# Layer 0 of a four-layer graph network: copies of nodes on ScalarE, later weights and transposes at other gates, another order of norms

## The chip, the cores and the metric

The kernel runs on one core of a Trainium2 chip. A core has a matrix engine (TensorE, in the profile PE, with its weight loads PEld), VectorE (DVE), ScalarE (ACT), GpSimd (POOL) and SyncE (SP), which here only issues DMAs. Each engine works through its own queue in order. They meet through semaphores. The metric is device microseconds of one execution, from the launch's start to its end.

## The reference, cut to what matters

The input `x` is 128 samples of 64 nodes with 256 features. Four layers follow each other, each as `x = x + layer(relu(layernorm(x)))`. The change lies in layer 0, which is two graph convolutions and then four LSTMs over windows of nodes:

```python
h = relu(einsum('ts,bsh->bth', adj, x @ Wg0 + bg0))
h = relu(einsum('ts,bsh->bth', adj, h @ Wg1 + bg1))
for p in range(1, 5):
    nw = 64 // p
    wins = h[:, :nw * p, :].reshape(B * nw, p, 256)
    last = lstm_last(Wih[p-1], Whh[p-1], bih[p-1], bhh[p-1], wins)   # gates i, f, g, o
    h = h.at[:, arange(nw) * p + (p - 1), :].set(last.reshape(B, nw, 256))
```

So a window of `p` nodes is read by `p` LSTM steps, and the last hidden state is written back in the place of the window's last node. The next `p` reads what the one before it wrote. Layers 1 to 3 (attention over edges, a graph convolution with batch norms, dense attention) are not touched.

## The kernel before

The 8192 rows (128 samples by 64 nodes) are cut into 16 chunks of 512 and 4 groups of 2048. All is 32-bit float. Layer 0 has two stages.

The first stage is `graph_convolutions(n)`, a generator for each chunk with five steps: the norm of the chunk (`Norm(...).all()`), the aggregation with the adjacency matrix, the two products with weights, and the second aggregation. A loop starts one generator in each round and takes every generator under way one step on, the oldest first, and from the fourth round on also one step of the generators that make tables for the later layers (`edge_tables`, `late_tables`). `Norm` takes statistics on DVE (L87, L88), then the root and the shift: for chunk 0 with a square root on ScalarE and two small instructions on DVE (L95 to L97), for the others with four small instructions on POOL (L99 to L102). Then four activations on ScalarE write the normed rows (L109). The results of the first half of the chunks stay in SBUF (`hTs0`, shown as `hT`), those of the second half go to DRAM (`hmem`).

The second stage runs the LSTMs. It has two halves of two groups each, `ga` and `gb`, and in each half four phases, one for each window length 1 to 4. A phase is a list of `Step`s: one time step `t` of one part of the nodes. Two parts alternate, so that one step's hidden state can be made while the other one multiplies. A step has three gates at `t` = 0 (nothing is fed back yet) and four after. The product of 256 by 256 features is done in 2x2 blocks by seven products instead of eight (a scheme of Strassen and Winograd): for this, weights and operands have to be summed and subtracted ahead. `Weights` loads 1 MB of weights on SP and makes four sums on POOL (L417): `wih` and `sih` for the input, in two buffers, `whh` and `shh` for the fed-back state, in one. `Step.prepare` makes the operands of a step (`xop`, two buffers): two copies of nodes on POOL (L606 and L607, for window length 1 not needed) and three subtractions on DVE (L608, L614, L615).

A gate's seven products go into three banks of PSUM: `pa` (three buffers), `pb` (two, shared with `bank`) and `pc` (three). Products 1, 6, 5 and 3 run into `pa` one after the other. Between them ScalarE reads `pa` (L668 after 1, L673 after 6) and DVE (L678 after 5), so the next product waits for that reader. The activations are L653, the tanh of the cell is L705. `gate` is a generator in four parts, and a loop over slots interleaves three gates: in a slot the newest gate runs products 1 and 2, the one before it product 5, the oldest 3 and 4, and the newest 6 and 7. So a gate is done two slots after it began. The last multiplication of a window's last step (L718) writes the nodes back.

In the same loop `prepare` of the next step is called in a step's next to last gate, `phase_over` loads later weights once a phase's last gate is done, and `group_out` is called for both chunk pairs of a group when its last step of window length 4 is done: it transposes the group back on TensorE (L152, 16 transposes for each chunk pair, which here is `c` = 0 or 1), adds it to the residual `x` (L155, loaded to `xres` by `fetch_x`), stores it to `xa` from POOL's queue, and loads the second half's `hT` over it from `hmem` on SP.

The order in each queue is not simply that of the text: a scheduler places instructions when it expects their operands and buffers to be ready, and takes the earlier one of the text where several are ready. `late(ins)` pins an instruction to its place in the order of the text.

Of the kernel before, what the change touches and what calls it, by code (L numbers as in the profile page):

```python
# [13 lines left out]
ALU = mybir.AluOpType  # L14
# [9 lines left out]
NEG = -1.0e30  # L24
# [6 lines left out]
def gnn_stack_kernel(ctx: ExitStack, tc: tile.TileContext, a: dict, out: bass.AP):  # L31
    nc = tc.nc
    NTOK = out.shape[0]
    NCH = NTOK // CHUNK
# [36 lines left out]
    def late(ins):  # L71

        tc.keep_in_program_order(ins)
# [72 lines left out]
    def add_transposed(xt, i0, src, col):  # L146

        p = bank()
        for i2 in range(2):
            for c in range(2):  # L150
                k = (i2 * 2 + c) * P
                nc.tensor.transpose(  # L152
                    p[:, k : k + P], src[:, c, col + i2 * P : col + (i2 + 1) * P], ident
                )
        nc.vector.tensor_tensor(  # L155
            xt[:, i0 : i0 + 2, :],
            p.rearrange("p (i d) -> p i d", i=2),
            xt[:, i0 : i0 + 2, :],
            ALU.add,
        )  # L160
# [9 lines left out]
    def late_tables():  # L170
        with ExitStack() as setup:
            s2 = setup.enter_context(tc.tile_pool(name="s2", bufs=1, side="right"))
            nc.sync.dma_start(out=wext[:, :, :D], in_=a["W3"])
            w3T = s2.tile([P, 2, D], F32, tag="w3T", name="w3T")
            nc.sync.dma_start(out=w3T, in_=a["W3T"])
            a3 = s2.tile([P, 2, 2], F32, tag="a3", name="a3")
            nc.sync.dma_start(out=a3, in_=a["a3"])

            nc.vector.tensor_scalar(mask3, adj2, 0.0, NEG, ALU.is_equal, ALU.mult)
            yield  # L180

            eye = s2.tile([P, T], F32, tag="eye", name="eye")
            for h in range(2):
                r = slice(h * T, (h + 1) * T)
                nc.vector.tensor_copy(eye[r, :], ident[r, r])
            an = s2.tile([P, T], F32, tag="an", name="an")
            anT = s2.tile([P, T], F32, tag="anT", name="anT")
            nc.vector.tensor_tensor(an, adj2, eye, ALU.add)
            nc.vector.tensor_tensor(anT, adjT2, eye, ALU.add)
            yield  # L190
            deg = s2.tile([P, 3], F32, tag="deg", name="deg")
            diag = s2.tile([P, T], F32, tag="diag", name="diag")
            nc.vector.tensor_tensor(diag, an, eye, ALU.mult)
            nc.vector.tensor_reduce(deg[:, 0:1], anT, AX.X, ALU.add)
            nc.vector.tensor_reduce(deg[:, 1:2], an, AX.X, ALU.add)
            nc.vector.tensor_reduce(deg[:, 2:3], diag, AX.X, ALU.add)
            yield
            dinv = s2.tile([P, 1], F32, tag="dinv", name="dinv")
            nc.vector.tensor_tensor(dinv, deg[:, 0:1], deg[:, 1:2], ALU.add)
            nc.vector.tensor_tensor(dinv, dinv, deg[:, 2:3], ALU.subtract)  # L200
            nc.gpsimd.tensor_tensor(dinv, dinv, half_power[:, 0:1], ALU.pow)
            yield
            dinv_b = s2.tile([P, P], F32, tag="dinv_b", name="dinv_b")
            nc.vector.tensor_copy(dinv_b, dinv.to_broadcast([P, P]))
            nc.vector.memset(bdH, 0.0)
            nc.vector.tensor_scalar(anT, anT, dinv, None, ALU.mult)
            yield
            p = bank()
            mm(p[:, :T], dinv_b[:T, :], ident[:T, :T])
            yield  # L210
            for h in range(2):
                r = slice(h * T, (h + 1) * T)
                nc.vector.tensor_tensor(bdH[r, r], p[r, :T], anT[r, :], ALU.mult)
            yield

            p = bank()
            for c in range(2):
                for k in range(2):
                    mm(
                        p[:, 2 * c : 2 * c + 2],  # L220
                        w3T[:, k, c * P : (c + 1) * P],
                        a3[:, k, :],
                        k == 0,
                        k == 1,
                    )
            yield
            for c in range(2):
                nc.vector.tensor_copy(wext[:, c, D:], p[:, 2 * c : 2 * c + 1])
                nc.vector.tensor_copy(wa2[:, c, :], p[:, 2 * c + 1 : 2 * c + 2].to_broadcast([P, T]))
            yield  # L230
# [160 lines left out]
    with ExitStack() as l0:  # L391
# [35 lines left out]
        weights = {}  # L427


        with ExitStack() as conv:  # L430
# [37 lines left out]
            nc.sync.dma_start(out=bias2, in_=a["bhh"])  # L468
            for h in range(2):
                r = slice(h * T, (h + 1) * T)  # L470
                nc.vector.tensor_copy(bdA[r, r], adjT2[r, :])

            rsum = wc.tile([P, T], F32, tag="rsum", name="rsum")
            p = bank()
# [3 lines left out]

            def graph_convolutions(n):

                h = Norm(coming.pop(n), n == 0).all()
                if 4 <= n + 3 < NCH:
                    coming[n + 3] = load_x(n + 3)
                yield
# [53 lines left out]
            for n in range(NCH + 4):  # L538
                if n < NCH:
                    under_way.append(graph_convolutions(n))  # L540
                for one in list(under_way):
                    if next(one, 0) == 0:
                        under_way.remove(one)
                    if n >= 3:
                        next(tables, None)
                if n == 2:
                    weights["ih", 0], weights["ih", 1] = Weights("ih", 1), Weights("ih", 2)
                    weights["hh", 1] = Weights("hh", 2)
                    nc.vector.tensor_tensor(bias, bias, bias2, ALU.add)
# [19 lines left out]
        class Step:  # L569
# [21 lines left out]
            def prepare(self):  # L591

                N, t = self.N, self.t
                x = xop.tile([P, 7 * NMAX], F32, tag="x", name="xop")
                if self.w == 1:
                    v = x[:, : 4 * N].rearrange("p (q n) -> p q n", n=N)
                    nc.vector.tensor_tensor(
                        v[:, 0:2], self.nodes(slice(2, 4), 0), self.nodes(slice(0, 3, 2), 0), ALU.subtract
                    )
                    b11, b21, b22 = (self.nodes(slice(k, k + 1), 0)[:, 0] for k in (0, 1, 3))  # L600
                    nc.vector.tensor_tensor(v[:, 2], b22, v[:, 0], ALU.subtract)
                    nc.vector.tensor_tensor(v[:, 3], b21, v[:, 2], ALU.subtract)
                    self.x = {1: b11, 2: b21, 3: b22, 4: v[:, 3], 5: v[:, 0], 6: v[:, 2], 7: v[:, 1]}
                    return
                v = x[:, : 7 * N].rearrange("p (q n) -> p q n", n=N)
                nc.gpsimd.tensor_copy(self.as_nodes(v[:, 0:2]), self.nodes(slice(0, 2), t))  # L606
                nc.gpsimd.tensor_copy(self.as_nodes(v[:, 2:3]), self.nodes(slice(3, 4), t))  # L607
                nc.vector.tensor_tensor(  # L608
                    self.as_nodes(v[:, 3:5]),
                    self.nodes(slice(2, 4), t),  # L610
                    self.nodes(slice(0, 3, 2), t),
                    ALU.subtract,
                )
                nc.vector.tensor_tensor(v[:, 5], v[:, 2], v[:, 3], ALU.subtract)  # L614
                nc.vector.tensor_tensor(v[:, 6], v[:, 1], v[:, 5], ALU.subtract)  # L615
                self.x = {1: v[:, 0], 2: v[:, 1], 3: v[:, 2], 4: v[:, 6], 5: v[:, 3], 6: v[:, 5], 7: v[:, 4]}
# [160 lines left out]
        def phase_over(ph):  # L777

            if ph + 2 < len(phases):
                weights["ih", ph + 2] = Weights("ih", phases[ph + 2])  # L780
            nxt = ph + 1 if ph + 1 < len(phases) and phases[ph + 1] > 1 else ph + 2
            if phases[ph] > 1 and nxt < len(phases):
                weights["hh", nxt] = Weights("hh", phases[nxt])

        tasks = [(s, q, k) for s in range(len(steps)) for k, q in enumerate(steps[s].gates)]
        flight = []
        later = []
        norm_steps = iter(())
        steps[0].prepare()
        for slot in range(len(tasks) + 2):  # L790
# [16 lines left out]
            if new:  # L807
                next(one)
                flight.append((new, one))
                at, k = new[0], new[2]  # L810
                if k == len(step.gates) - 2 and at + 1 < len(steps):
                    steps[at + 1].prepare()
                if step.w == MAX_SKIP and step.t == 2 and k < 2:
                    for u in range(2):
# [2 lines left out]
            while later and later[0][0] <= slot:  # L817
                _, kind, n = later.pop(0)
                residual[n] = fetch_x(n)
            next(norm_steps, None)  # L820
            if old:
                (at, q, k), step = old[0], steps[old[0][0]]
                if k == len(step.gates) - 1:
# [10 lines left out]
                            norms1[n] = Norm(xt)  # L834
                        norm_steps = first_norms1(norms1)
                    if step.w == MAX_SKIP and step.t == MAX_SKIP - 1:
                        for c in range(2):
                            group_out(step.g, c)
        for _ in norm_steps:
            pass  # L840
    psums["banks"] = None
    w12 = ctx.enter_context(tc.tile_pool(name="w12", bufs=1, side="right"))
    xin1 = l01.enter_context(tc.tile_pool(name="xin1", bufs=2, side="right"))
# [667 lines left out]
```

## Time and profile before

| | us |
|---|---|
| median of three runs (lowest to highest) | 2181.02 (2179.18 to 2182.44) |
| the profiled execution | 2181.59 |
| its span, first to last instruction | 2179.8 |

The stages by time, with the busy time of each engine in them (us, from the same execution):

| from to | what | PE | DVE | ACT | POOL | granted PE clock |
|---|---|---|---|---|---|---|
| 0 to 34 | start of the convolutions | 21.36 | 17.35 | 9.46 | 17.49 | 0.95 |
| 34 to 206 | convolutions | 172.00 | 113.48 | 68.31 | 26.64 | 1.00 |
| 206 to 763 | LSTMs, first half | 538.91 | 324.95 | 296.27 | 84.88 | 0.98 |
| 763 to 1311 | LSTMs, second half | 531.00 | 321.31 | 293.83 | 85.21 | 0.98 |
| 1311 to 2180 | layers 1 to 3 | 811.90 | 493.32 | 426.17 | 200.32 | 0.94 to 0.98 |

How to read it: PE is busy nearly all the time, so what a change can win on the other engines counts only where PE stands still for it, or where the granted clock falls below 1 because PE stood still. A matmul on 256 columns is recorded as two instructions of 0.216 us each at full clock.

### The profile page before, as it was taken

How to read it: one execution, taken by the hardware profiler on the slowest of the kernel's cores; microseconds unless marked ns; L12 is line 12 of the kernel's file. 1: busy time of each engine (PE TensorE's matmuls, PEld its weight loads, DVE VectorE, ACT ScalarE, POOL GpSimd, SP SyncE). 2: the span in 40 equal slices, each digit the busy share in tenths (PEclk: the TensorE clock that was granted, in tenths of full speed). 3: DMA queues.
4: the chain of work that ended last, by engine and by line, in shares of the span. 5: the costliest groups of instructions: out<-in, count | busy, mean ns of one | idle time of the engine just before them, and what ended most of it. 6: DMA issues, size and time to landing. Idle time of an engine off the chain costs nothing.

```text
span 2179.8 us, 25495 instructions
## 1 busy us (share of the span) xinstructions
PE 2075.2 (95%) x9508; PEld 1373.7 (63%) x9508; DVE 1270.4 (58%) x2281; ACT 1094.0 (50%) x2079; POOL 414.5 (19%) x567
## 2 busy tenths in 40 slices
PE   7999999999899899999999989999998989999898
PEld 5776488766688647876668873333344745444686
DVE  6665665655555666655455555667665455333676
ACT  3344766544544376654455535566563445460444
POOL 4110010300310111122020201121220221000662
PEclk9999999999999999999999999999999989999899
DMA  8331000100100420010010043122315741022012
GB/s 283 98 101 50 0 20 1 39 1 1 39 1 0 173 97 20 1 39 0 1 39 1 1 131 107 58 73 87 83 61 148 209 136 48 1 77 77 29 60 68
DMA packets 93740, 134.02 MB, mean 61 GB/s; under 512 B 6320, under 2 KB 81968, under 8 KB 91312
## 3 DMA queue, kind: packets, MB, share of 16 engines
q1 hardware_dynamic: 87456, 108.59, 14.8%
q0 software_dynamic: 5552, 23.60, 3.7%
q8 instruction: 75, 1.23, 0.2%
q14 instruction: 49, 0.40, 0.1%
q10 hardware_dynamic: 608, 0.20, 0.0%
HBM read 86.75 MB, written 45.61 MB: 61 GB/s over the span
## 4 chain that ended last, share of the span: by engine, by line
PE 85%; DVE 4%; POOL 3%; DMA 3%; ACT 3%; issue 1%; ACTq 0%; SPq 0%; POOLq 0%; DVEq 0%
PE pa L625 26%; PE bank L50 20%; PE pair L50 17%; PE pc L625 12%; PE pb L625 6%; DMA xb<-xo 1%; ACT gate L653 1%; POOL sih L417 1%; PE bank L152 1%; POOL shh L417 1%; PE bank L1076 1%; DMA xo<-xa 1%; PE pair L1341 1%; PE pair L1309 1%; DVE hT L718 1%
## 5 line engine op out<-in xcount | busy, mean ns | idle before, releaser
L653 ACT ACTIVATE gate<-gate,bias 128x256 f32<-128x256 f32 (+2 forms) x368 | 248.3, 678 | 226.4 <-DVE gate L669 118.6
L625 PE MATMUL pa<-xop,sih 128*128 128x256 f32 (+2 forms) x1056 | 352.2, 423 | 5.9 <-ACT gate L668 3.5
L625 PEld LDWEIGHTS pa<-xop,sih 128*128 128x128 f32 x1056 | 202.1, 193 | 81.0 <-issue 23.3
L625 PE MATMUL pc<-xop,wih 128*128 128x256 f32 (+2 forms) x736 | 252.3, 425 | 0.0
L606 POOL COPY xop<-hT 128x512 f32<-128x512 f32 (+1 forms) x44 | 60.3, 1371 | 803.3 <-issue 411.2
L625 PE MATMUL pa<-lstm_h,shh 128*128 128x256 f32 (+1 forms) x672 | 212.7, 398 | 0.0
L934 DVE SCALAR_TENSOR_TENSOR lr<-lr 128x1024 f32<-128x1024 f32 x128 | 152.1, 1218 | 86.3 <-ACT lr L933 86.0
L669 DVE TENSOR_TENSOR gate<-pb,gate 128x256 f32<-128x256 f32 (+2 forms) x184 | 87.4, 475 | 159.5 <-PE pb L625 122.9
L625 PEld LDWEIGHTS pc<-xop,wih 128*128 128x128 f32 x736 | 141.2, 192 | 52.1 <-issue 23.4
L683 DVE TENSOR_TENSOR gate<-pc,gate 128x256 f32<-128x256 f32 (+2 forms) x184 | 87.4, 475 | 107.4 <-PE pc L625 106.3
L625 PEld LDWEIGHTS pa<-lstm_h,shh 128*128 128x128 f32 x672 | 127.7, 190 | 30.2
L933 ACT COPY lr<-pair 128x1024 f32<-128x1024 f32 x128 | 125.0, 1015 | 34.3 <-PE pair L50 34.3
L625 PE MATMUL pc<-lstm_h,whh 128*128 128x256 f32 (+1 forms) x448 | 141.8, 398 | 0.0
L668 ACT COPY gate<-pa 128x256 f32<-128x256 f32 (+2 forms) x184 | 76.9, 418 | 125.1 <-PE pa L625 124.5
L653 ACT ACTIVATE gate<-pa,bias 128x256 f32<-128x256 f32 (+2 forms) x184 | 94.5, 514 | 85.7 <-PE pa L625 85.6
L50 PE MATMUL pair<-sd_hot,xq 64*128 64x512 f32 x512 | 134.4, 622 | 0.3 <-ACT lr L933 0.3
L50 PE MATMUL bank<-wlv,hT 128*128 128x512 f32 x256 | 122.7, 611 | 7.0 <-ACT hT L141 7.0
L109 ACT ACTIVATE h<-xin,ln_nm,ln_rs 128x256 f32<-128x256 f32 x184 | 97.0, 592 | 42.5 <-POOL ln_nm L102 42.1
L50 PE MATMUL pair<-h,w2T 128*128 128x512 f32 x256 | 112.2, 601 | 5.3 <-ACT h L1260 5.3
L50 PE MATMUL pair<-aggT,w1T 128*128 128x512 f32 x256 | 112.4, 593 | 0.4 <-DVE aggT L1233 0.4
L625 PE MATMUL pb<-xop,wih 128*128 128x256 f32 (+1 forms) x320 | 103.6, 408 | 7.6 <-POOL xop L606 7.6
L625 PE MATMUL pa<-xop,wih 128*128 128x256 f32 (+1 forms) x320 | 103.0, 404 | 8.0 <-POOL xop L606 6.0
(257 smaller groups left out, 3628.5 us busy)
## 6 DMA issues: line engine op xcount, KB each, us to landing
field<-sd_hot SPq DMA_DIRECT2D x8, 1152.0 KB, 10.9
wih<-in_WihT SPq DMA_DIRECT2D x8, 1024.0 KB, 4.8
xres<-in_x SPq DMA_DIRECT2D x16, 512.0 KB, 5.8
xa<-xres POOLq DMA_DIRECT2D x16, 512.0 KB, 5.0
xo<-xa SPq DMA_DIRECT2D x16, 512.0 KB, 4.6
dense<-field POOLq DMA_DIRECT2D x8, 1024.0 KB, 9.8
xb<-xo SPq DMA_DIRECT2D x16, 512.0 KB, 5.1
xin<-xb SPq DMA_DIRECT2D x16, 512.0 KB, 3.9
```

The lines of the kernel that those rows point to most:

```text
L50: nc.tensor.matmul(o, lhsT, rhs, start=start, stop=stop)
L109: nc.scalar.activation(self.h[:, i, :], self.xt[:, i, :], AF.Relu, bias=self.nm[:, i : i + 1], scale=self.rs[:, i : i + 1],)
L152: nc.tensor.transpose(p[:, k : k + P], src[:, c, col + i2 * P : col + (i2 + 1) * P], ident)
L417: nc.gpsimd.tensor_tensor(o, x, y, op)
L606: nc.gpsimd.tensor_copy(self.as_nodes(v[:, 0:2]), self.nodes(slice(0, 2), t))
L625: ins = nc.tensor.matmul(p[:, : self.N], weights[kind, self.phase](k, q), x[k], start=first_ and kind == "ih", stop=kind == "hh" or not se ...
L653: nc.scalar.activation(out, in_, AF.Tanh if q == 2 else AF.Sigmoid, bias=bias[:, self.w - 1, 2 * q + j : 2 * q + j + 1],)
L668: nc.scalar.copy(blk[0, 0], pa[:, :N])
L669: nc.vector.tensor_tensor(blk[0, 0], pb[:, :N], blk[0, 0], ALU.add)
L683: nc.vector.tensor_tensor(blk[1, 0], pc[:, :N], blk[1, 0], ALU.add)
L933: nc.scalar.copy(lr, p)
L934: nc.vector.scalar_tensor_tensor(lr, lr, 0.2, lr, ALU.mult, ALU.max)
```

## The change

Seven edits, all in layer 0 or the tables made beside it. (1) The two copies of nodes in `prepare` run on ScalarE instead of POOL. (2) `phase_over` puts the load of the input weights of the phase after next on a list, and the loop makes it eight slots later; the weights of the fed-back state stay where they were. (3) `group_out` of a group's two chunk pairs runs one and two slots after its last gate instead of at once, at a fixed place at the slot's end, and the first of each four transposes is pinned to the order of the text. (4) `prepare` of the first step of window length 1 in the second half moves from the next to last to the last gate of the step before, since it reads what `group_out` loads. (5) In the loop of the convolutions the newest chunk's generator goes first. (6) All norms of layer 0 take the root on ScalarE. (7) The two copies that build `bdA` go to POOL, and the making of `mask3` is pinned to the order of the text. Copies, sums, transposes and loads are the same in number as before.

```diff
@@ add_transposed
-                nc.tensor.transpose(
+                ins = nc.tensor.transpose(
                     p[:, k : k + P], src[:, c, col + i2 * P : col + (i2 + 1) * P], ident
                 )
+                if k == 0:
+                    late(ins)
@@ late_tables
-            nc.vector.tensor_scalar(mask3, adj2, 0.0, NEG, ALU.is_equal, ALU.mult)
+            late(nc.vector.tensor_scalar(mask3, adj2, 0.0, NEG, ALU.is_equal, ALU.mult))
@@ convolutions
-                nc.vector.tensor_copy(bdA[r, r], adjT2[r, :])
+                nc.gpsimd.tensor_copy(bdA[r, r], adjT2[r, :])
...
-                h = Norm(coming.pop(n), n == 0).all()
+                h = Norm(coming.pop(n), True).all()
...
-                for one in list(under_way):
+
+                for one in under_way[-1:] + under_way[:-1] if n < NCH else list(under_way):
@@ Step.prepare
-                nc.gpsimd.tensor_copy(self.as_nodes(v[:, 0:2]), self.nodes(slice(0, 2), t))
-                nc.gpsimd.tensor_copy(self.as_nodes(v[:, 2:3]), self.nodes(slice(3, 4), t))
+                nc.scalar.copy(self.as_nodes(v[:, 0:2]), self.nodes(slice(0, 2), t))
+                nc.scalar.copy(self.as_nodes(v[:, 2:3]), self.nodes(slice(3, 4), t))
@@ phase_over
-                weights["ih", ph + 2] = Weights("ih", phases[ph + 2])
+                later_weights.append((slot + 8, ph + 2))
...
+        later_weights = []
...
-        later = []
+        later, outs = [], []
@@ loop over slots
+                while outs and outs[0][0] <= slot:
+                    group_out(*outs.pop(0)[1:])
+
+                new_half = at + 1 < len(steps) and at and steps[at + 1].w == 1 < step.w
-                if k == len(step.gates) - 2 and at + 1 < len(steps):
+                if k == len(step.gates) - (1 if new_half else 2) and at + 1 < len(steps):
                     steps[at + 1].prepare()
...
+            while later_weights and later_weights[0][0] <= slot:
+                _, ph = later_weights.pop(0)
+                weights["ih", ph] = Weights("ih", phases[ph])
...
-                        for c in range(2):
-                            group_out(step.g, c)
+                        outs += [(slot + 1, step.g, 0), (slot + 2, step.g, 1)]
...
+        for _, g, c in outs:
+            group_out(g, c)
```

In the changed kernel the lines are a little further down: L606 and L607 become L609 and L610, L614 and L615 become L617 and L618, L625 becomes L628, L668 becomes L671, L653 becomes L656, L718 becomes L721 and L417 becomes L419; L152 stays.

## The prediction

> **What bounds the kernel now.** I read the page's parts 1 and 2 first, then TensorE's waits over layer 0 (the change touches nothing after it; from the first projection of layer 1 on, the built order of instructions is the same on all five engines), then the timelines of POOL, PE, DVE and ACT at the longest of these waits, and last ScalarE's groups by shape.
>
> ```profile
> PE 2075.2 (95%) x9508; PEld 1373.7 (63%) x9508; DVE 1270.4 (58%) x2281; ACT 1094.0 (50%) x2079; POOL 414.5 (19%) x567
> ```
>
> TensorE is busy 95% of the span, so only its idle time and the time at a lower clock can be won. Its waits from 0 to 1311 us, which is layer 0 (who waited for whom, us in total, times, longest):
>
> ```profile
> PE bank L152 <- DVE hT L718: 11.3, 4, 5.4
> PE bank L50 <- ACT h L109: 9.3, 3, 5.3
> PE pb L625 <- POOL xop L606: 7.6, 3, 2.8
> PE pa L625 <- POOL xop L606: 6.0, 2, 3.3
> PE pa L625 <- ACT gate L668: 3.5, 6, 1.0
> PE pa L625 <- ACT gate L653: 2.1, 6, 0.4
> ```
>
> Three families: the first norms (L109), the node copies of `prepare` on POOL (L606), and the transposes of `group_out` behind the last multiplication of a group (L718). The two longest of the second family, on POOL and then on PE (start, us, what, idle before):
>
> ```profile
> 572.20 1.48 POOL L417 TENSOR_TENSOR sih<-wih 128x512 f32<-128x512 f32 x1 [25.03 <-DMA wih<-in_WihT]
> 573.63 1.92 POOL L606 COPY xop<-hT 128x512 f32<-128x512 f32 x1
> ...
> 584.94 2.11 POOL L417 TENSOR_TENSOR shh<-whh,shh 128x512 f32<-128x512 f32 x1
> 587.00 1.07 POOL L606 COPY xop<-hT 128x512 f32<-128x512 f32 x1
> ```
>
> ```profile
> 571.67 0.59 PE L625 MATMUL pc<-xop,wih 128*128 128x256 f32 x2
> 575.60 1.22 PE L625 MATMUL pa<-xop,wih 128*128 128x256 f32 x2 [3.34 <-POOL xop L606]
> ...
> 588.13 1.22 PE L625 MATMUL pb<-xop,wih 128*128 128x256 f32 x2 [2.84 <-POOL xop L606]
> ```
>
> The copies stand in POOL's queue behind sums of weights that no matmul needs yet. And a pair of matmuls that takes 0.59 us takes 1.22 after the stall: the clock has halved.
>
> [...] gaps of 2.4 us and more are followed by half rate, those of 1.56 us are not. [...] the subtraction L614 of 128x256 takes 1.48 us at 576.2 beside POOL and 0.42 alone. [...] So a copy that waits on ScalarE holds all behind it; before, it held only POOL.
>
> **The change part by part**, against the profiled execution (2181.59 us, span 2179.8; 0.6 above the median, within the runs' spread).
>
> *Copies of nodes on ScalarE* (44 steps, two copies each). Price: ScalarE's copies of the same sizes from PSUM take 0.37 us (128x256), 0.43 (128x336) and 0.58 (128x512). The slope (0.58-0.37)/256 gives an estimate of 0.71 for 128x672. So 0.95 us a step for windows of two and four (32 steps), 1.14 for three (12), against 2.05 and 2.51 on POOL (1.30+0.74, 1.55+0.96). Strided reads by ScalarE from SBUF are not in the trace: from below the same, from above POOL's price; I take the same.
>
> What goes: PE's five waits on L606, 2.40+3.34+2.84 in the first half and 2.39+2.62 in the second, 13.6 us; and the half rate behind them. At 575.60 twelve matmul records take 5.21 us where 0.216 each makes 2.6: 2.6 lost. In the same way 1.5 is lost at 588.13, 1.7 each at 430.60 and at its twin near 987, and 2.9 at 1131.44. That is 10.4. The waits on ScalarE just ahead of 428 and 985 (0.99+0.42, 0.99+0.41) come from DVE's L614 and L683 being late behind POOL: 2.8. Together 26.8.
>
> What is late next: at each change from windows of three to four, the copy waits for L718, which ends at 572.62; with 0.1 to start and 0.58 to run, PE waits 1.1 us instead of 3.34 (and of 2.62)[...]. The subtractions L614 and L615 still run beside POOL's sums (1.48 and 1.15 against 0.42), about 1.0 again each time. At each change from two to three the copy waits on ScalarE for L718 (412.95 to 414.18) with two readers of `pa` behind it: 1.2. With 0.3 for the copy in place of the wait at 588, 2x1.1+2x1.0+2x1.2+0.3 = 6.9 stays. Net gain 19.9.
>
> What it costs: in a three-gate stretch (t = 0) ScalarE has little room. From 344 to 358 it is busy 11.8 of 14 us; its copy L673 must read `pa` before product 5 adds to it, four products (1.7 us) after product 4. In these lie an activation (0.72) and L673 (0.36): 0.6 free, and a step's copies are 0.95. So 0.35 is lost each time, more with a tanh (1.06) in the way: I take 0.5, two sets in a stretch, 1.0. That is for the second pair of windows of two; at the change from one to two (ScalarE busy 37.0 of 50 us from 200 to 250) 1.25. Both in each half: 4.5 lost. The stretches of three and four are in the 6.9. In four-gate steps eight products (3.45 us) stand in place of four: nothing lost. Bounds: 0 to 12.
>
> *Weights of later phases eight gates later*: four loads of 1 MB and sixteen sums on POOL are asked for later. But the built order has the same sequence of `wih` and `whh` on SP and on POOL as before (`wih` ahead of `whh` at every phase change), because the scheduler places each as soon as its buffer is free. So I count nothing. If the queue had followed the text, `shh` would be ready some 6 us earlier; with the copies gone from POOL it is ready at about 583 to 585, and its first matmul comes some 4 us after the first of its step, near 586. Cover: thin, 1 to 3 us; if it is gone, 1 to 2.
>
> *Last transposes one and two gates later.* Before, PE waited 1.56, 2.71 and 1.56 us for L718, and at half rate 1.0 more (group out 756.73 to 763.17 is 6.4 us, the one at 724.29 is 5.4). With a gate of 6.05 us between, L718 is long done: 6.8 gained. The fourth wait (5.42, end of the layer) stays. What moves with it: 16 transposes, 8 adds, 4 stores on POOL and 4 loads of `hT` on SP for each group. SP's order puts two `xres` loads, each waiting for a store, between the two chunks' `hT` loads. Chunk 0: transposes end near 731.5, landing takes 5.3 us (3.5 to 8.0), first product near 740: covered by 1 to 3 us. At the end of the layer `xres` of chunk 1 lands some 1304 us, its add starts near 1305: covered, barely; if not, below 1 us.
>
> *Start.* `mask3` leaves its place ahead of the second statistics' aggregate (DVE idle 1.04 us for `adj`) and two copies of 0.19 go to POOL: first norm 1.2 earlier. Chunk 1's statistics now follow chunk 0's at about 7 us instead of 14.46, and its roots take 0.7 on ScalarE and DVE (7.82 to 8.52 shows it) instead of 2.0 on POOL (17.29 to 19.27). This closes waits of 2.52 and 1.52 and the half rate at 21 us (1.7). Sum 6.9 at most; [...] I take 4.5 (2 to 6.9). Sixteen roots and 32 small DVE instructions, and one more table load (1.28 us at 4.37) after the logarithm, lie under PE, which has no gap from 34 to 206 us with ScalarE at 40%.
>
> Sum: 19.9 - 4.5 + 6.8 + 4.5 = 26.7. 2181.6 - 26.7 = 2154.9, taken as 2155.
>
> **The rivals.** (a) *ScalarE becomes the bound; slower.* Each step's copies hold PE for their whole length: 32x0.95+12x1.14 = 44 us, against 31.2 gained elsewhere (19.9+6.8+4.5): 2181.6+12.8 = 2194. It decides from 0.7 us a step (31.2/44). For: ScalarE's 84% in the stretch above, strict order. Against: four-gate steps have room, and gates already take a tanh of 1.06 us without a PE gap.
>
> (b) *The next waiter takes over.* DVE beside POOL's sums, and `shh` still behind `sih`, keep half of the 19.9 (10), the start brings 2.5, the groups 5.5, ScalarE costs 6.5: 11.5 gained, 2170. For: the unchanged order of weights. Against: `shh` at 587 was behind two node copies.
>
> (c) *Late `hT` loads.* If landing takes 8 us behind stores, the second half's first products wait 2 and lose 3 to the clock: 2160.
>
> (d) *No effect*: gains and ScalarE's cost cancel; needs 0.6 to 0.8 us a step.
>
> **How the numbers follow.** Forecast (2146 to 2163, with c) 0.64; b (2163 to 2176) 0.26; d 0.03; a 0.07. The range 2146 to 2171 holds about 0.8. A measurement here can tell 0.2%, 4.4 us, from no change: faster 0.90, same 0.03, slower 0.07.
>
> **What would show it.** Right: no PE wait on `xop` above 1.5 us; half rate only at the start, at most once near 570 and 1130, and at the layer's end; no PE wait on L721 before the last one; PE waits on ScalarE's gate instructions (L668, L653, L673) up from 7.0 to about 13 us. Wrong: these waits above 30 us in total, or `lstm_h,shh` matmuls waiting for POOL.

## The result and the profile after

| | before | after |
|---|---|---|
| median (lowest to highest), us | 2180.34 (2179.18 to 2182.44) | 2159.8 (2157.8 to 2160.59) |
| ratio after to before | | 0.9903, 95% interval 0.9886 to 0.992 |
| span of the profiled execution, us | 2179.8 | 2158.8 |

So the change wins about 20.5 us; the forecast was 2155. Part 1 of the page of the changed kernel:

```profile
PE 2062.0 (96%) x9508; PEld 1368.2 (63%) x9508; DVE 1270.5 (59%) x2309; ACT 1157.3 (54%) x2183; POOL 299.5 (14%) x421
```

POOL has 115 us less to do, ScalarE 63 us more, and PE is busy 13 us less with the same 9508 matmuls: fewer of them ran at half rate (the mean granted clock is 0.986 against 0.979). What is left of PE's waits in layer 0 (who waited for whom, us in total, times, longest):

```profile
PE pa L628 <- ACT gate L676: 8.6, 12, 1.5
PE bank L152 <- DVE xres L157: 5.8, 7, 3.6
PE bank L152 <- DVE hT L721: 5.5, 1, 5.5
PE bank L50 <- ACT h L109: 3.9, 1, 3.9
...
PE pa L628 <- ACT xop L609: 3.1, 2, 1.5
PE pa L628 <- ACT gate L656: 1.7, 2, 0.9
PE bank L50 <- DVE aggT L132: 1.7, 1, 1.7
...
PE pa L628 <- ACT gate L671: 1.4, 4, 0.4
```

Against the list of before: `xop` fell from 13.6 to 3.1, the write-back `hT` from 11.3 to the one wait at the layer's end, the first norms (L109) from 9.3 to 3.9. The waits on ScalarE's gate instructions (L676, L656, L671) rose from 7.0 to 11.7. The waits for `xres` grew from 1.8 us in seven pieces (L155 before, none above 0.3) to 5.8, of which 3.6 in one piece.

That piece lies where the first half of the LSTMs gives way to the second. DVE's timeline there (start, us, instruction, idle before):

```profile
719.41 0.42 DVE L681 TENSOR_TENSOR gate<-pa,gate 128x256 f32<-128x256 f32 x1 [0.37 <-PE pa L628]
722.62 1.23 DVE L600 TENSOR_TENSOR xop<-hT 128x1024 f32<-128x1024 f32 x1 [2.79 <-DMA hT<-hm]
723.76 0.42 DVE L686 TENSOR_TENSOR gate<-pc,gate 128x256 f32<-128x256 f32 x1
724.10 0.68 DVE L604 TENSOR_TENSOR xop<-hT,xop 128x512 f32<-128x512 f32 x1
724.81 0.69 DVE L605 TENSOR_TENSOR xop<-hT,xop 128x512 f32<-128x512 f32 x1
725.42 1.22 DVE L696 TENSOR_TENSOR gate<-gate 128x1024 f32<-128x1024 f32 x1
726.56 1.28 DVE L157 TENSOR_TENSOR xres<-bank,xres 128x512 f32<-128x512 f32 x2
```

and PE's:

```profile
722.66 1.04 PE L152 MATMUL bank<-ident,hT 128*128 128x128 f32 x8
727.29 1.97 PE L152 MATMUL bank<-ident,hT 128*128 128x128 f32 x8 [3.60 <-DVE xres L157]
729.05 1.92 PE L628 MATMUL pa<-hT,wih 128*128 128x512 f32 x2
```

L600 is the first subtraction of `prepare` for the first step of the second half (a step of window length 1, which reads `hT` straight). It stands on DVE ahead of the additions L157 of the second chunk pair, and waits there for `hT`, which lands at 722.6. The additions hold the two `bank` buffers, so the third group of transposes waits 3.60 us. Then the clock halves: the granted clock is 0.50 from 725.8 to 732.6, eight transposes take 1.97 us where the same eight take 1.26 in e1 below, and two products of 512 columns 1.92 instead of 1.02. The chain of waits of the changed kernel shows the load on the path (start, us):

```profile
716.83 5.67 DMA hT<-hm
```

Where the gain accrued, from the start of the same matmul in both traces: 5.5 us before the first LSTM matmul (198.4 and 192.9), 9.3 more by the end of the first half's phases, nothing over its two `group_out` (where 5.3 had been forecast), 6.2 more in the second half's phases, about 2 more by the first product of layer 1. That product starts at 1311.9 before and at 1289.0 after, 22.9 us earlier. Layers 1 to 3 then give back 2.1: from there to the last matmul they took 861.7 us before and 863.8 after.

### The profile page after: what moved, and what is told of

It reads as the page before. It is cut to its first block, busy times and chain, and to the rows that moved or that the text cites. A ratio compares the mean times of both kernels' runs of the same rounds, so it can differ in the third digit from the quotient of the medians.

```text
span 2158.8 us, 25368 instructions
## 1 busy us (share of the span) xinstructions
PE 2062.0 (96%) x9508; PEld 1368.2 (63%) x9508; DVE 1270.5 (59%) x2309; ACT 1157.3 (54%) x2183; POOL 299.5 (14%) x421
## 4 chain that ended last, share of the span: by engine, by line
PE 80%; ACT 5%; issue 4%; DMA 4%; DVE 4%; POOL 1%; ACTq 0%; SPq 0%; POOLq 0%; DVEq 0%
PE pa L628 24%; PE bank L50 19%; PE pair L50 16%; PE pc L628 12%; PE pb L628 6%; DMA xb<-xo 2%; ACT gate L656 1%; ACT gate L708 1%; PE bank L1088 1%; PE pair L1353 1%; PE pair L1321 1%; ACT h L109 0%; ACT xop L609 0%; DMA xin<-xb 0%; PE pair L1068 0%
## 5 line engine op out<-in xcount | busy, mean ns | idle before, releaser
L628 PE MATMUL pa<-xop,sih 128*128 128x256 f32 (+2 forms) x1056 | 347.9, 418 | 10.3 <-ACT gate L676 8.6
L656 ACT ACTIVATE gate<-gate,bias 128x256 f32<-128x256 f32 (+2 forms) x368 | 246.9, 678 | 182.1 <-DVE gate L672 98.0
L628 PEld LDWEIGHTS pa<-xop,sih 128*128 128x128 f32 x1056 | 199.9, 191 | 84.2 <-issue 20.6
L628 PE MATMUL pc<-xop,wih 128*128 128x256 f32 (+2 forms) x736 | 251.5, 423 | 0.0
L628 PE MATMUL pa<-lstm_h,shh 128*128 128x256 f32 (+1 forms) x672 | 213.0, 399 | 0.0
L628 PEld LDWEIGHTS pc<-xop,wih 128*128 128x128 f32 x736 | 140.4, 191 | 51.1 <-issue 22.4
L628 PEld LDWEIGHTS pa<-lstm_h,shh 128*128 128x128 f32 x672 | 127.8, 190 | 30.0
L628 PE MATMUL pc<-lstm_h,whh 128*128 128x256 f32 (+1 forms) x448 | 142.0, 399 | 0.0
L50 PE MATMUL pair<-sd_hot,xq 64*128 64x512 f32 x512 | 134.5, 622 | 0.4 <-ACT lr L945 0.3
L656 ACT ACTIVATE gate<-pa,bias 128x256 f32<-128x256 f32 (+2 forms) x184 | 94.6, 514 | 72.0 <-PE pa L628 71.0
L671 ACT COPY gate<-pa 128x256 f32<-128x256 f32 (+2 forms) x184 | 76.9, 418 | 104.5 <-PE pa L628 103.8
L50 PE MATMUL bank<-wlv,hT 128*128 128x512 f32 x256 | 122.8, 612 | 7.0 <-ACT hT L141 7.0
L50 PE MATMUL pair<-h,w2T 128*128 128x512 f32 x256 | 112.5, 603 | 5.3 <-ACT h L1272 5.3
L50 PE MATMUL pair<-aggT,w1T 128*128 128x512 f32 x256 | 112.5, 593 | 0.1
L681 DVE TENSOR_TENSOR gate<-pa,gate 128x256 f32<-128x256 f32 (+2 forms) x184 | 87.4, 475 | 35.4 <-PE pa L628 33.1
L628 PE MATMUL pa<-xop,wih 128*128 128x256 f32 (+1 forms) x320 | 102.1, 401 | 5.0 <-ACT xop L609 3.1
L109 ACT ACTIVATE h<-xin,ln_nm,ln_rs 128x256 f32<-128x256 f32 x184 | 97.0, 592 | 12.3 <-DVE ln_nm L97 8.5
L628 PE MATMUL pb<-xop,wih 128*128 128x256 f32 (+1 forms) x320 | 101.1, 400 | 0.0
```

The source lines that it names most:

```text
L50: nc.tensor.matmul(o, lhsT, rhs, start=start, stop=stop)
L109: nc.scalar.activation(self.h[:, i, :], self.xt[:, i, :], AF.Relu, bias=self.nm[:, i : i + 1], scale=self.rs[:, i : i + 1],)
L628: ins = nc.tensor.matmul(p[:, : self.N], weights[kind, self.phase](k, q), x[k], start=first_ and kind == "ih", stop=kind == "hh" or not se ...
L656: nc.scalar.activation(out, in_, AF.Tanh if q == 2 else AF.Sigmoid, bias=bias[:, self.w - 1, 2 * q + j : 2 * q + j + 1],)
L671: nc.scalar.copy(blk[0, 0], pa[:, :N])
L681: nc.vector.tensor_tensor(blk[1, 1], pa[:, :N], blk[1, 1], ALU.add)
```

## The experiments

Each kernel is the changed kernel with the edit shown. All have layers 1 to 3 in the same order, yet these took between 862.3 and 869.9 us, mostly alike among kernels measured together. So beside the ratio against the kernel before, measured together with each, I give the start of the first product of layer 1 (L50 `bank<-wlv,hT`) in the trace: it measures layer 0 alone.

| kernel | ratio to before | 95% interval | layer 1 starts at, us |
|---|---|---|---|
| before | 1 | | 1311.9 |
| after | 0.9903 | 0.9886 to 0.992 | 1289.0 |
| e1_prep_after_adds | 0.9866 | 0.985 to 0.9883 | 1282.4 |
| e2_copies_on_pool | 0.9961 | 0.9947 to 0.9975 | 1303.2 |
| e3_groups_at_once | 0.9904 | 0.9887 to 0.992 | 1291.0 |
| e4_start_undone | 0.9932 | 0.9915 to 0.9949 | 1296.3 |
| e5_weights_at_once | 0.9901 | 0.9886 to 0.9916 | 1287.7 |
| e6_copies_doubled | 0.9957 | 0.9942 to 0.9972 | 1299.8 |
| e7_windows_of_two_on_pool | 0.9902 | 0.9888 to 0.9915 | 1286.0 |
| e8_three_mends | 0.9884 | 0.9869 to 0.9899 | 1284.3 |
| e9_eight_steps | 0.9935 | 0.9922 to 0.9949 | 1295.3 |
| e10_first_steps_of_two_on_pool | 0.9882 | 0.9867 to 0.9897 | 1284.5 |
| e11_roots_on_pool | 0.993 | 0.9914 to 0.9947 | 1293.6 |
| e12_prep_again | 0.9887 | 0.9872 to 0.9902 | 1285.4 |

**e1_prep_after_adds: the new wait.**

```diff
@@ Step.prepare
-                    nc.vector.tensor_tensor(
+                    (late if (self.g, self.b0) == (2, 0) else id)(nc.vector.tensor_tensor(
                         v[:, 0:2], self.nodes(slice(2, 4), 0), self.nodes(slice(0, 3, 2), 0), ALU.subtract
-                    )
+                    ))
```

> Only one instruction of the changed kernel is held to the order of the text: the first subtraction of `prepare` (L600) for the first step of the second half, so that DVE does it after the additions L157 of group_out instead of ahead of them. Theory 1 (DVE's strict order): in the changed kernel L600 waits on DVE for hT (landed at 722.6), the additions queue behind it, PE waits 3.6 us for their PSUM buffer and then runs at half rate. With L600 behind them that wait falls to 0.35, the half rate near 726 goes, and 3.25 + about 2.5 = 5.7 us are won: 2154. Theory 2 (DMA is late, whatever the order on DVE): PE then waits as long at the first product that reads hT or xop, 0 to 1 us are won: 2159.

Only DVE's order changes, around this one instruction. DVE in this kernel:

```profile
721.62 1.23 DVE L696 TENSOR_TENSOR gate<-gate 128x1024 f32<-128x1024 f32 x1 [0.79 <-ACT gate L656]
722.76 1.28 DVE L157 TENSOR_TENSOR xres<-bank,xres 128x512 f32<-128x512 f32 x2
724.19 1.29 DVE L157 TENSOR_TENSOR xres<-bank,xres 128x512 f32<-128x512 f32 x2
725.40 1.22 DVE L600 TENSOR_TENSOR xop<-hT 128x1024 f32<-128x1024 f32 x1
```

PE's wait is 0.53 us, no half rate follows near 726 (two products of 512 columns take 1.02), and L600 finds its `hT` landed and waits for nothing. Theory 1 holds: it was the place in DVE's queue, not the load. Layer 0 ends 6.6 us earlier than in the changed kernel.

**e12_prep_again: the same kernel again.**

> The kernel of the first run again, beside the two kernels above on the same chip, to compare them directly: ratio 0.986 to 0.989.

The wait is 0.53 again; layer 0 ends 3.6 us earlier than in the changed kernel. The wait is gone for certain, while its worth varies: 2.4 to 6.6 us over the four pairs of e1 and e12 with the changed kernel and e5 (which has the same order), 4.5 in the mean. The ratios agree (0.9866 and 0.9887 against 0.9903 and 0.9901), though the intervals of e12 and the changed kernel overlap. Why the same stall costs different amounts was not shown; the last section has it with half rate behind it and without.

**e2_copies_on_pool: edit 1 undone.**

```diff
-                nc.scalar.copy(self.as_nodes(v[:, 0:2]), self.nodes(slice(0, 2), t))
-                nc.scalar.copy(self.as_nodes(v[:, 2:3]), self.nodes(slice(3, 4), t))
+                nc.gpsimd.tensor_copy(self.as_nodes(v[:, 0:2]), self.nodes(slice(0, 2), t))
+                nc.gpsimd.tensor_copy(self.as_nodes(v[:, 2:3]), self.nodes(slice(3, 4), t))
```

> The changed kernel with the node copies L609 and L610 back on POOL; all other edits stay. Theory 1 (the sum of the prediction, 19.9 - 4.5): 15.4 us slower, 2175, with PE waits on xop L609 of 13 us, half rate after them, and PE waits on the gate copies L676 down from 8.6 to about 3. Theory 2 (most of the stalls at the phase changes came from the early place of the weights' sums, which edit 2 moved): below 6 us slower, 2160 to 2166. Theory 3 (ScalarE's copies cost as much as they bring): within 2 us of 2160.

12.7 us slower by the ratios (0.0058 of 2186), 14.2 in layer 0. PE's waits on `xop` are back at 16.1 us (13.6 in the kernel before), and those on ScalarE's gate instructions fall from 11.7 to 6.3 (L676 from 8.6 to 1.2, while L671 rises from 1.4 to 3.5):

```profile
PE pb L628 <- POOL xop L609: 10.1, 4, 3.8
PE pa L628 <- POOL xop L609: 6.0, 2, 3.3
...
PE pa L628 <- ACT gate L676: 1.2, 6, 0.2
```

Theory 1 holds nearly in full, and edit 2, which this kernel keeps, does not spare the copies: POOL's timeline at the longest of these waits shows the copy behind the last sums of the weights as before.

```profile
576.54 2.14 POOL L419 TENSOR_TENSOR shh<-shh,whh 128x512 f32<-128x512 f32 x1
578.65 2.12 POOL L419 TENSOR_TENSOR whh<-whh 128x512 f32<-128x512 f32 x1
580.74 1.26 POOL L419 TENSOR_TENSOR shh<-whh,shh 128x512 f32<-128x512 f32 x1
581.94 1.08 POOL L609 COPY xop<-hT 128x512 f32<-128x512 f32 x1
```

**e3_groups_at_once: edits 3 and 4 undone.**

```diff
-                        outs += [(slot + 1, step.g, 0), (slot + 2, step.g, 1)]
+                        for c in range(2):
+                            group_out(step.g, c)
...
-                if k == len(step.gates) - (1 if new_half else 2) and at + 1 < len(steps):
+                if k == len(step.gates) - 2 and at + 1 < len(steps):
```

The pin of the transposes is taken out as well.

> The changed kernel with the chunk pairs' group_out at once again, without the pin of the transposes, and with prepare of the second half's first step at the next to last gate (edits 3 and 4 undone). The prediction's term: 6.8 us slower, 2166.6, with PE waits on L721 of 1.56, 2.71 and 1.56. Reading of the trace after: the move wins these but pays 3.6 + 2.5 at 724 to 733, so undoing it costs 0.7 to 2 us, 2160.5 to 2162; the wait on L157 of 3.6 and the half rate near 726 are gone.

The waits on the write-back are all back (its line is L719 here, that of the additions L155), and the 3.6 us on the additions are gone:

```profile
PE bank L152 <- DVE hT L719: 11.3, 4, 5.4
...
PE bank L152 <- DVE xres L155: 2.0, 8, 0.3
```

Layer 0 ends 2.0 us later than in the changed kernel, and the ratio is the same. The trace's reading holds, the prediction's term doesn't: the move won its 5.8 us of waits and paid most of it to L600. With L600 held back the term is whole: against this kernel e1 ends layer 0 8.5 us earlier and e12 5.6, where 6.8 had been forecast for the move.

**e4_start_undone: edits 5 to 7 undone.**

```diff
-                h = Norm(coming.pop(n), True).all()
+                h = Norm(coming.pop(n), n == 0).all()
...
-                for one in under_way[-1:] + under_way[:-1] if n < NCH else list(under_way):
+                for one in list(under_way):
```

and `mask3` and `bdA` as before.

> The changed kernel with the start as before: root on POOL from chunk 1 on, oldest chunk first, mask3 not pinned, bdA copied on DVE (edits 5 to 7 undone). The prediction's term: 4.5 us slower, 2164.3. The matmul of the LSTM that came first was 5.5 us earlier in the changed kernel, so by the trace 5.5 slower, 2165.3. Rival: what is won at the start is lost again later in layer 0 (the start of the LSTMs waits for something else), below 2 us.

The first LSTM matmul starts at 200.1 instead of 192.9, 7.2 us later, and 7.3 are left at the start of layer 1. The gain of the start is not lost again.

**e11_roots_on_pool: edit 6 alone undone.**

```diff
-                h = Norm(coming.pop(n), True).all()
+                h = Norm(coming.pop(n), n == 0).all()
```

> The changed kernel with edit 6 alone undone: roots on POOL from chunk 1 on, while chunk 1's statistics stay early and mask3 stays off the way. The prediction gave the root 1.3 us (0.7 on ScalarE and DVE against 2.0 on POOL) of 4.5 for the whole start: the first LSTM matmul 1 to 2 us later. Rival: the early statistics only pay with the root on ScalarE, 4 us and more of the 5.5 to 7.2 go.

The rival is right: 5.7 us of the start go with this edit alone (first LSTM matmul at 198.6), and 4.6 are left at the start of layer 1. The largest new wait shows how, on POOL, ScalarE and PE in turn:

```profile
43.00 0.23 POOL L102 TENSOR_SCALAR ln_nm<-ln_nm 128x4 f32<-128x4 f32 x1
```

```profile
43.27 2.07 ACT L109 ACTIVATE h<-xin,ln_nm,ln_rs 128x256 f32<-128x256 f32 x4 [12.56 <-POOL ln_nm L102]
45.25 1.13 ACT L503 ACTIVATE h1T<-h1T 128x512 f32<-128x512 f32 x2
```

```profile
45.91 2.30 PE L50 MATMUL bank<-wg,h1T 128*128 128x256 f32 x6 [3.37 <-ACT h1T L503]
```

With the newest chunk's norm first, ScalarE has its four activations L109 ahead of the older chunk's L503. They wait for POOL's root, so L503 waits behind them, and PE behind L503; half rate follows at 46.8 (these six products take 2.30 us; in the changed kernel fourteen of the same size take 3.29 at 42.39). In the order that edit 5 makes, a late root also holds up the older chunk. No run undoes edit 5 or edit 7 alone, so how the rest of the start divides among them is not shown.

**e5_weights_at_once: edit 2 undone.**

```diff
-                later_weights.append((slot + 8, ph + 2))
+                weights["ih", ph + 2] = Weights("ih", phases[ph + 2])
```

> The changed kernel with edit 2 undone: phase_over loads the input weights at once again. The built order of instructions is the same on all five engines as with the edit. The prediction's term: 0, so the time of the changed kernel, ratio 0.990 against the kernel before and the same PE waits within 0.2 us. Rival: the load's place in the text decides when shh is ready, and PE waits on POOL's L419 of 1 us and more show up: 2161 to 2163.

The same time: 0.9901 against 0.9903. Edit 2 changes nothing. Since its order is that of the changed kernel, it also shows how far two executions of one order differ in layer 0: 1.3 us at its end, up to 3.6 on the way.

**e6_copies_doubled: is ScalarE the bound?**

```diff
-                nc.scalar.copy(self.as_nodes(v[:, 0:2]), self.nodes(slice(0, 2), t))
+                for _ in range(2):
+                    nc.scalar.copy(self.as_nodes(v[:, 0:2]), self.nodes(slice(0, 2), t))
```

> The changed kernel with the larger of the two node copies (L609) run twice in each of the 44 steps: ScalarE has 16 x 0.67 + 28 x 1.14 = 43 us more to do, 28 us of it in steps with four gates. Theory 1 (ScalarE binds only in three-gate stretches and at the changes of phase, 16 steps at t = 0): the 28 steps at t above 0 lose nothing, and of the 16 (8 x 0.67 + 8 x 1.14 = 14.5 us) half to all is lost, 7 to 15 us. Rival a (ScalarE's copies hold PE in every step): 35 to 43 us slower.

12.1 us slower in layer 0 than e5, with 43 us more on ScalarE. Over the stretches of windows of three and four in which only steps with four gates copy (437 to 550, 600 to 706 and their twins, 14 doubled copies, 16.0 us) 0.6 us is lost. Most of the rest goes at the changes of phase, and about 2 us in the second pair of windows of two:

```profile
PE pa L629 <- ACT xop L610: 6.2, 2, 3.1
PE pb L629 <- ACT xop L610: 5.8, 10, 1.3
```

Theory 1 holds and rival a is out: ScalarE's copies cost next to nothing under steps with four gates. Where they are called in a step with three gates, most of all at the changes of phase, they cost time.

**e7_windows_of_two_on_pool and e10_first_steps_of_two_on_pool: where ScalarE is tight.** In e7 all 16 steps of windows of two copy on POOL; e10 is e1 with only those at `t` = 0 there.

```diff
-                nc.scalar.copy(...)
+                (nc.gpsimd.tensor_copy if self.w == 2 else nc.scalar.copy)(...)
```

> The changed kernel with the copies of windows of two on POOL (16 steps); windows of three and four keep them on ScalarE. In the kernel before no PE wait on xop lay in the steps of windows of two. Theory 1 (the prediction's ScalarE term of 4.5 lies there): the PE waits on L676 fall from 8.6 to some 4 or less, and the last matmul of the LSTMs comes 3 to 5 us earlier. Theory 2 (these waits come from the gates' own copies and activations, not from the node copies): within 1 us of the changed kernel. Theory 3 (POOL's copies slow DVE, which then is late for PE): slower by 1 to 3 us.

> The kernel of the first run, with the copies of only the steps at t = 0 of windows of two on POOL (8 steps), all others on ScalarE. Theory 1 (ScalarE binds in the three-gate stretch that follows the copies of t = 0): the PE waits on L676 fall as with all of them on POOL, from 8.4 to about 4, and the wait of 1.5 on POOL's copy behind the sums of the weights stays: 1 to 3 us faster than the kernel of the first run. Theory 2 (copies of t = 1, called in the last gates of the three-gate step ahead, are what binds): waits on L676 stay above 6, within 1 us.

In e7 the waits on L676 halve as theory 1 has it, but others take their place:

```profile
PE pa L628 <- ACT gate L676: 4.2, 9, 1.4
...
PE pb L628 <- POOL xop L609: 1.5, 1, 1.5
```

Layer 0 ends 1.7 us earlier than in e5 and 3.0 earlier than in the changed kernel, and the ratio is the same. The last LSTM matmul, which the expectation went by, comes 2.2 us earlier than in e5 and 3.4 earlier than in the changed kernel. In e10, against e12 on the same chip, L676 falls from 10.0 to 4.5, L656 rises from 1.9 to 4.4, and 0.8 us is won in layer 0; against e1, the same kernel as e12, 2.1 us are lost. The expected wait on POOL's copy did not come. So theory 1 holds for the waits on L676, and the time won is not clear of the spread between two executions of one order. The copies are a part of these waits, but not all of it. The largest of them in the changed kernel, 1.50 us at 282.2, has other instructions just ahead of the copy it waits for:

```profile
279.79 1.06 ACT L708 ACTIVATE gate<-lstm_c 128x1024 f32<-128x1024 f32 x1 [0.78 <-DVE lstm_c L707]
280.75 1.10 ACT L656 ACTIVATE gate<-gate,bias 128x256 f32<-128x256 f32 x2
281.76 0.35 ACT L676 COPY gate<-pa 128x256 f32<-128x256 f32 x1
```

**e9_eight_steps: which copies needed to leave POOL.** e1 with ScalarE only for `t` = 0 of windows of three and four (`self.w > 2 and t == 0`).

> The kernel of the first run (the changed kernel with one subtraction held behind the additions of group_out), and the node copies on ScalarE only in the eight steps at t = 0 of windows of three and four; the 36 other steps copy on POOL as in the kernel before. Theory 1 (all that the edit brings lies in these eight steps, where the copies stood behind sums of weights on POOL; elsewhere the place of the copies doesn't matter, apart from windows of two): within 2 us of the run with windows of two on POOL after the subtraction's 3.5 to 6 us, that is a ratio of 0.986 to 0.988, and no PE wait on xop above 1.6. Theory 2 (freeing POOL from the other copies matters too, since DVE is slow beside it): 3 to 6 us slower than the kernel of the first run.

Both theories miss: 10.0 us slower in layer 0 than e12, with PE waits on POOL of 1.58, 2.40, 3.73 and 3.80 us. POOL's order shows the reason, which is my choice of steps:

```profile
577.39 1.26 POOL L419 TENSOR_TENSOR shh<-whh,shh 128x512 f32<-128x512 f32 x1
578.59 1.07 POOL L609 COPY xop<-hT 128x512 f32<-128x512 f32 x1
```

Copies are called one step ahead, so the one that stands behind all eight sums belongs to the third step of a phase, the first at `t` = 1. The two waits for steps at `t` = 0 (3.34 and 2.62 before) fell to about 1.6 with their copies on ScalarE. So the gain of edit 1, as far as this run shows, lies in the first copies after a phase's weights come in, those at `t` = 1 among them. Whether twelve such steps suffice was not tried.

**e8_three_mends: e1, e7 and the bias sum together.** At the start of the changed kernel PE waits 1.73 us for `aggT`, because DVE does the sum of the biases (L552), which waits for a load until 14.1, ahead of a copy (L132). This kernel pins that sum to a later round.

```diff
-                    nc.vector.tensor_tensor(bias, bias, bias2, ALU.add)
+                if n == 6:
+                    late(nc.vector.tensor_tensor(bias, bias, bias2, ALU.add))
```

> The changed kernel with three mends together: the first subtraction of the second half's first step held behind the additions of group_out (6.3 us won alone), the copies of windows of two on POOL (3 to 5 if theory 1 of the run before holds), and the sum of the two biases (L552), which waits for in_bhh until 14.1 us on DVE with a PE wait of 1.7 on aggT behind it, held to a later round of the convolutions (1 to 2). Sum 10 to 13 us faster than the changed kernel, ratio 0.984 to 0.986 against the kernel before. Rival: one wait hides the other, 7 us and less.

The wait on L552 is gone and the first LSTM matmul comes no earlier (193.7): PE waits 0.63 and 1.79 us near 40 for L503 (once 1.48 in the changed kernel), which is again queued behind L109. Layer 1 starts at 1284.3, between e1 (1282.4) and e12 (1285.4), so the two further mends bring nothing that could be measured. The rival holds. Of all kernels here e1 (and e12), e8 and e10 are the fastest, 0.987 to 0.989 of the kernel before, and the runs do not tell them apart.

## Why the prediction was right, and where it was off

The forecast was 2155 with a range of 2146 to 2163; 2159.8 lies in it. The main mechanism is the one that was named, but the terms were not all of the right size, and one step was wrong.

*The bound and the copies: right, one price wrong.* PE's waits on `xop` were to fall from 13.6 to 2.2, and fell to 3.1; no half rate is left at 430, 587, 987 and 1130, but one stretch is left near 565, where two products of 256 columns take 1.06 us instead of 0.59. Of the net 15.4 (19.9 less 4.5), undoing the edit shows 14.2; rival b, by which 3.5 of it would be left (10 less 6.5), is out. The mis-sized term is the price of a step's copies: 0.95 us for windows of two and four, 1.14 for three, taken from ScalarE's reads of PSUM. Measured: 1.10 for windows of two, 1.80 for four and 1.81 for three. That is 68 us of copies in place of 44. It cost little, because steps with four gates hide it (e6), but it shows at the change to windows of four: 1.11 and 0.66 in place of 0.58 and 0.37, and PE waits 1.53 where 1.1 was forecast.

```profile
563.89 1.11 ACT L609 COPY xop<-hT 128x512 f32<-128x512 f32 x1
564.91 0.66 ACT L610 COPY xop<-hT 128x256 f32<-128x256 f32 x1
```

*ScalarE's cost in stretches of three gates: right in sign, too high.* The waits on its gate instructions rose to 11.7 (13 forecast), but moving the copies of windows of two away wins 1.7 to 3.0 us in layer 0 (e7) and nothing certain in e10, not 4.5; other waits take over.

*Weights: right.* Same order, same time. `shh` was ready at 577.7, and its first matmul started at 580.7: the thin cover of 1 to 3 us was 3.

*The last transposes: this step failed.* 6.8 us were forecast, 2.0 are there (e3). The three waits of 1.56, 2.71 and 1.56 went, as said. What failed is "Chunk 0: transposes end near 731.5, landing takes 5.3 us (3.5 to 8.0), first product near 740: covered by 1 to 3 us". The load took 5.7, as said, but the first product is not its first reader. With edits 3 and 4 `prepare` is called between the two chunk pairs of the group, and its subtraction L600 was DVE's next instruction at 719.8, about 5 us before the first product could have come. The text asked what is queued behind a waiting instruction on ScalarE, and did not ask it for DVE. The trace of before showed the first reader: the same subtraction, L597 there, already waited for `hT` on DVE, but behind the additions (L155), where it held up nothing that PE needed:

```profile
732.69 1.23 DVE L597 TENSOR_TENSOR xop<-hT 128x1024 f32<-128x1024 f32 x1 [2.09 <-DMA hT<-hm]
```

Rival c had the cause (the `hT` load) and a like price (2 and 3 us; it became 3.6 and about 2.5) in another place.

*The start: right in sign, too low.* 4.5 forecast, 5.5 measured directly and 7.2 by undoing. The root was given 1.3 of it and carries 5.7 (e11): early norms put L109 ahead of L503 on ScalarE, and PE's wait for L503 is 3.37 us with the root on POOL and 1.48 with it on ScalarE.

*Layers 1 to 3: counted at nothing, 2.1 lost.* DVE's statistics L87 wait 3.86 us for `xin` at 1303.9 where they waited 0.94, a copy (L934) queues behind them, and PE waits 1.10. This lies within what these layers differ by from run to run.

Sum, undone one by one: 14.2 + 2.0 + 7.3 = 23.5, close to the 22.9 by which layer 0 became shorter; less 2.1 in the layers after, it is close to the span's 21.0. The forecast's 26.7 is too high by the groups (4.8), the copies (1.2) and the later layers (2.1), and too low by the start (1.0 to 2.8). The start's error hides part of the others, which is luck.

*Signs named ahead.* Right: no wait on L721 before the last, no `shh` matmul waiting on POOL, waits on ScalarE far below 30. Just missed: waits on `xop` of 1.53 and 1.52 against a limit of 1.5. Wrong: the half rate near 726 was on no list.

## What to carry to other kernels

When a step moves, list every instruction that it issues and find, on each in-order engine, what then stands behind the first reader of its transfer; the matmul may be the second reader. Moving an instruction to another engine paid here where its old queue made PE wait for it (e2, e9), and not where it only ran faster on the new engine (the windows of two, e7). One subtraction held to its place was worth some 4.5 us of layer 0; taking the copies of 16 steps back to POOL gave 1.7 to 3.0, which the ratio does not show. Judge an edit inside a long kernel by the start of one fixed instruction in the trace, since the rest of the kernel can differ by more than the edit.

## What the runs showed of the hardware that had not been expected

*The length of one gap did not tell whether half rate follows.* My reading of before had it so: half rate (a granted clock of 0.5) after gaps of 2.4 us and more, none after those of 1.56. In the changed kernel the gap of 3.60 us at 723.7 was followed by 6.8 us at half rate; in e7 the gap at the same place was 3.37 us long, and none followed (eight transposes in 1.26 us, two products of 512 columns in 1.02). In the changed kernel itself the granted clock fell to 0.50 after the gap of 1.53 us that ended at 565.05, and stayed at 1.00 after the gap of 1.52 us that ended at 1112.58:

```profile
565.05 0.94 PE L628 MATMUL pa<-xop,wih 128*128 128x256 f32 x2 [1.53 <-ACT xop L609]
565.79 1.06 PE L628 MATMUL pb<-xop,wih 128*128 128x256 f32 x2
...
1112.58 0.70 PE L628 MATMUL pa<-xop,wih 128*128 128x256 f32 x2 [1.52 <-ACT xop L609]
1113.11 0.60 PE L628 MATMUL pb<-xop,wih 128*128 128x256 f32 x2
```

What else decides was not shown. Executions of one order differed at this stall too: e5 was 1.2 us ahead of the changed kernel when the third group of transposes began, and 3.6 when the changed kernel's stretch at half rate was over.

*The copies of nodes took longer four apart than two apart, on ScalarE and POOL alike.* On ScalarE 512 elements took 0.65 to 0.69 us when two apart in SBUF and 1.10 to 1.16 when four apart. POOL's best values were like these (0.65 and 1.07 in the kernel before), but others there went up to 1.14 and 2.06, with means of 0.83 and 1.77. Estimated from two sizes each, ScalarE's copies take (0.67 - 0.43)/256 = 0.94 ns for an element at 8 bytes and (1.14 - 0.66)/256 = 1.88 at 16, twice as much; POOL's best copies take (0.65 - 0.41)/256 = 0.94 and (1.07 - 0.62)/256 = 1.76. So ScalarE's copies were as fast as POOL's best and faster than its mean, but by e7 and e9 it was the queue that counted.
